# One gate convolution on Trainium2: its 144 input rows split as 128 rows times three shifts plus 16 rows loaded three times shifted

## The chip, the cores and the metric

The kernel runs on one core of one Trainium2 chip. The metric is the device time of one execution in microseconds (us). Three executions of the kernel before took 12310.65, 12336.9 and 12346.97 us; the median is 12336.9 us.

## The reference, cut to what matters

The input x has 32 images of 8 channels and 256x256 pixels. Two layers follow each other. Only layer 0 matters for the change; layer 1 is a group norm and a quantised 3x3 convolution of what layer 0 gives.

```
drive = gn(x); grid = drive
for _ in range(15):                                   # the lattice
    mapped = 3.9 * grid * (1 - grid)
    local = conv3x3_depthwise(mapped, K_local)
    grid = 0.85 * (0.7 * mapped + 0.3 * local) + 0.15 * drive
cml = clip(grid, 1e-4, 1 - 1e-4)
h   = relu(conv3x3(gn(x), Wp, bp))                    # the NCA: 8 -> 128 channels
nca = sigmoid(conv1x1(h, Wu, bu))                     # 128 -> 8
gin = concat([gn(x), cml, nca])                       # the gate: 24 channels
g   = sigmoid(conv1x1(relu(conv3x3(gin, Wg1, bg1)), Wg2, bg2))
y   = x + g * cml + (1 - g) * nca
```

The change touches `conv3x3(gin, Wg1, bg1)`, the gate's first convolution, 24 channels to 8.

## The kernel before, in words

**Groups.** The 32 images go in eight groups of four. The lattice of a group runs one channel of its four images at a time, 15 steps each, in two halves of two images (`half`, products at L499). While the lattice of group g runs, the products of the other stages are put between its halves: the NCA of the same group (`hidden` L585, `drain` L601), the gate of group g-1 (`gate`), and the group norm of group g+1. So the first group's lattice has no gate beside it, the next seven have 32 gate tiles each beside them, and the gates of the last four images stand alone at the end, before layer 1.

**Order.** The generators at the end of the stage write the order of TensorE's products by hand: each yields a weight, and `together` and `both` take the next piece from the one that is behind. The weights of the gate are not changed. The order on the other engines, and on the queue of DMA issues on SP, is not the program's: a planner with a cost model orders them by its own due times. So one tile's loads need not stand together on SP. Phase columns: the lattice leaves its columns sorted by phase, position q*64+j for column 4j+q, so that a shift by one column is a move by 64 positions for three phases and a move by 192 and one position for the fourth. This is why `PARTS` has five pieces for three shifts: 256, 192+63 and 192+63 columns.

**One gate tile** is 32 image rows, 8 tiles for each image, 256 in all. It works on eight blocks of four output rows. A block needs six input rows of 8 channels, 48 partitions for each of x, lattice and NCA. `inputs` (L656 to L665) loads them from the scratch `gs_s` in DRAM with three DMAs: x and lattice into `gin` (96 partitions), NCA into `gnc` (48 partitions), both from a pool with two buffers. The convolution (L758 to L768) then makes for each of the two sources, each of the five parts and each of four groups of 32 output partitions one product: 2 x 5 x 4 = 40. All of them read at most 512 columns in float32 and accumulate in one half of a PSUM tile. `S.activation` at L770 takes the sum into `r1`; the 1x1 convolution of the tile before (`opened`, L714 and L716) stands in PE's order just ahead of the 40 products, and the first of these waits for the activation L716.

**Loads and who needs them.** SP issues the tile's loads `gin`, `gnc` (L662), the tile's `mix` (L672), the NCA's `im` (L566), the store of y (L734), the lattice's loads and stores (L462), and the lattice's exchange of edge rows (L474 and L475, `m_a<-m_a`). The exchange comes after every second half: VectorE writes `m_a`, SP issues two small DMAs, and a half two places later on PE reads what they moved. SP takes its instructions strictly one after the other, in the order that the planner gave them.

Of the kernel before, what the change touches and what calls it, by code (L numbers as in the profile page):

```python
# [31 lines left out]
F32 = mybir.dt.float32  # L32
# [8 lines left out]
P = 128  # L41
C = 8
# [12 lines left out]
PART = PROWS * C * W  # L55
# [15 lines left out]
NT8 = 8  # L71
# [38 lines left out]
def kernel(  # L110
# [6 lines left out]
    wp: bass.AP,  # L117
    wu: bass.AP,
    wg1: bass.AP,
    wg2: bass.AP,  # L120
    w1: bass.AP,
    bp: bass.AP,
# [3 lines left out]
    nc = tc.nc  # L126
    B = x.shape[0]
    V, S, G, T = nc.vector, nc.scalar, nc.gpsimd, nc.tensor

    def dram_ap(t, offset, dims):  # L130
        return bass.AP(t.tensor, t.offset + offset, dims)


    cp = ctx.enter_context(tc.tile_pool(name="const", bufs=1))
# [8 lines left out]
    grp = cp.tile([P, 4], F32, name="grp")  # L143
    mean_x = cp.tile([P, B, 4], F32, name="mean_x")
    rstd_x = cp.tile([P, B, 4], F32, name="rstd_x")
    gw = cp.tile([96, 2, 3, 32], F32, name="gw")
    gw2 = cp.tile([P, P], F32, name="gw2")
    qw = cp.tile([P, 3, P], BF16, name="qw")
    wp_hi = cp.tile([P, 3, HID], F32R, name="wp_hi")
# [16 lines left out]
    with tc.tile_pool(name="prep", bufs=1) as pp, tc.tile_pool(name="prep2", bufs=2) as pp2:  # L166
# [3 lines left out]
        kc = pp.tile([P, 3, P], F32, name="kc")  # L170
        nc.sync.dma_start(kc, kcen)
        nc.sync.dma_start(gw, wg1)
        g2 = pp.tile([P, C], F32, name="g2")
        nc.sync.dma_start(g2, wg2)
        wl = pp.tile([P, 72], F32, name="wl")
# [79 lines left out]
    with ExitStack() as one:  # L255
# [7 lines left out]
        hp, xp, sp2, gp, gip = pool("hp", 4), pool("xp", 2), pool("sp2", 1), pool("gp", 3), pool("gip", 2)  # L263
# [4 lines left out]
        def unit():  # L268
            return ps_u.tile([P, 2, 512], F32, name="pt", tag="pt")
# [6 lines left out]
        fixed = lambda shape, name, dt=F32: np_.tile(shape, dt, name=name)  # L276
        hi, lo = fixed([P, 2, 2, W], "hi", F32R), fixed([P, 2, 2, W], "lo", F32R)
        ims = [fixed([P, 2, 8, PW], f"im{i}", F32R) for i in range(2)]
        for t in ims:
            for w in (0, PW - 1):  # L280
                G.memset(t[:, :, :, w].bitcast(F32), 0.0)
        TU = 2 * NT
        m_a = [fixed([P, TU, NJ + 2], f"m_a{i}") for i in range(2)]
        m_b = [fixed([P, TU, NJ + 1], f"m_b{i}") for i in range(2)]
        d_a = [fixed([P, TU, NJ], f"d_a{i}") for i in range(4)]
        d_b = [fixed([P, TU, NJ + 1], f"d_b{i}") for i in range(4)]
        for t in m_a:
# [104 lines left out]
        def lattice(g):  # L392
# [27 lines left out]
            def begin(ds, s):  # L420

                da, db = ds[s]
                for ts in (slice(0, 10), slice(10, TU)):
                    if s == 0:
# [55 lines left out]
            def half(c, step, s, d, m_a, m_b):  # L480
# [42 lines left out]
                if a2b:  # L523
                    edge = m_b[:, :, 0 : NJ + 1 : NJ]
                    G.tensor_tensor(edge, edge, junk.unsqueeze(1).to_broadcast([P, TU, 2]), ALU.mult)  # L525
                else:
# [129 lines left out]
        def inputs(b, t):  # L656

            src = gs_s[b % NBUF]
            gin = gip.tile([96, 8, W], F32, name="gin", tag="gin")
            gnc = gip.tile([48, 8, W], F32, name="gnc", tag="gnc")  # L660
            for j, to in enumerate((gin[:48], gin[48:], gnc)):
                nc.sync.dma_start(  # L662
                    to, dram_ap(src, j * PART + 32 * t * C * W, [[W, 48], [4 * C * W, 8], [1, W]])
                )
            return gin, gnc  # L665

        def blend(b, t):

# [25 lines left out]
        def begin_gate(b):  # L694
            return scales(b), (inputs(b, 0), blend(b, 0))

        PARTS = (
            (1, slice(0, 256), slice(0, 256)),
            (0, slice(64, 256), slice(0, 192)),
            (0, slice(1, 64), slice(192, 255)),  # L700
            (2, slice(0, 192), slice(64, 256)),
            (2, slice(192, 255), slice(1, 64)),
        )

        def gate(b):
# [36 lines left out]
            sc, ahead = staged.pop(b)  # L742
            last = None
            for t in range(NT8 + 1):
                while chores:
                    chores.pop(0)()
                now = {}
                two = unit()
                if last:
                    now["gt"] = opened(two[:, 1, :], last["r1"])  # L750
                    now["was"] = last
                if t < NT8:
                    (gin, gnc), mix = ahead
                    if t < NT8 - 1:
                        now["ahead"] = [inputs(b, t + 1)]
                    elif (b + 1) % GB:
                        staged[b + 1] = [inputs(b + 1, 0)]
                    pa = two[:, 0, :]  # L758
                    three = pa.rearrange("p (k w) -> p k w", w=W)
                    for j, src in enumerate((gin, gnc)):  # L760
                        rows_ = src.shape[0]
                        for n, (dx, to, of) in enumerate(PARTS):
                            for i in range(4):
                                T.matmul(  # L764
                                    three[32 * i : 32 * i + 32, :, to],
                                    gw[:rows_, j, dx, :], src[:, i::4, of],
                                    start=(j == 0 and n == 0), stop=(j == 1 and n == len(PARTS) - 1),
                                )  # L768
                    r1 = wk.tile([P, 512], F32, name="r1", tag="r1", bufs=1)
                    S.activation(r1, pa, AF.Relu, bias=bv[:, 0:1])  # L770
                    now["r1"], now["t"], now["mix"] = r1, t, mix

                def mix_(now):
                    was = now["was"]
                    was["y"] = mixed(now["gt"], *was["df"])

                def arrange_(now):
                    now["df"] = arrange(sc, now["mix"])

                def blend_(now):  # L780
                    if now["t"] < NT8 - 1:
                        now["ahead"].append(blend(b, now["t"] + 1))
                    elif (b + 1) % GB:
                        staged[b + 1] = scales(b + 1), (*staged[b + 1], blend(b + 1, 0))

                def measured_(now):
                    measured(now["was"]["t"], now["was"]["y"])

                def extremes_(now):
                    extremes(now["was"]["t"], now["was"]["y"])  # L790

                steps = []
                if last:
                    steps.append(mix_)
                if t < NT8:
                    steps += [arrange_, blend_]
                if last:
                    steps += [measured_, extremes_]
                chores.extend([lambda f=f, now=now: f(now) for f in steps])
                if sums:  # L800
                    chores.append(sums.pop(0))
                last = now
                yield 2.3 if t < NT8 else 0.9
                while t < NT8 - 1 and len(now.get("ahead", ())) < 2 and chores:
                    chores.pop(0)()
                ahead = now.get("ahead")
# [89 lines left out]
        for g in range(NG):  # L896
            fill, t = images(nca, g), T_NCA
            if g:
                fill, t = both(fill, t, after(g - 1, images(gate, g - 1)), T_GATE), t + T_GATE
            if g + 1 < NG:  # L900
                fill, t = both(fill, t, prep(g + 1), T_PREP), t + T_PREP
            if g == 0:
                fill, t = chain(prep(0, ((1,), (2,), (3,))), fill), t + 3.6
# [9 lines left out]
    with ExitStack() as two:  # L913
# [92 lines left out]
        for b in range(B + 1):  # L1006
# [5 lines left out]
            if last:  # L1012
                i, os_ = last
# [9 lines left out]
            if done:  # L1023
                i, os_ = done
# [53 lines left out]
```

## Time and profile before

The profiled execution of the kernel before took 12344.86 us; its span from first to last instruction is 12343.1 us.

| what | value |
|---|---|
| median of three executions | 12336.9 us |
| profiled execution, its span | 12344.86 us, 12343.1 us |
| TensorE busy | 11018.7 us, 89% of the span |
| VectorE busy | 7823.5 us, 63% |
| ScalarE, GpSimd busy | 3787.1 us (31%), 1577.6 us (13%) |
| mean granted TensorE clock | 0.950 |
| DMA queue of SP | 2380096 packets, 65.1% of 16 engines' span |
| stretch with lattice and gates side by side (1630 to 11396 us): TensorE, DMA share | 9164.00 of 9766.00 us, 0.69 |
| last gates alone (11396 to 11790 us): TensorE, DMA share | 314.41 of 394.00 us, 0.87 |

A line of the costliest groups reads: source line, engine, operation, what is written and read, shape (rows*columns of the array, then partitions x elements), count, and behind the bar busy time and mean time of one, then the engine's idle time before them and what ended it. A float32 product stands in the records as two instructions, so the gate's 40 products of a tile are 80 records.

### The profile page before, as it was taken

What the parts mean: (1) busy time and instruction counts of PE and PEld (TensorE: products, weight loads), DVE (VectorE), ACT (ScalarE), POOL (GpSimd) and SP (SyncE); (2) the same over time, 40 slices, a digit from 0 to 9 for tenths busy, and PEclk for the clock granted to TensorE, in tenths of its full rate; (3) what the DMA queues carried; (4) which work ended last, traced back from release to release, by engine and by line L of the source; (5) the groups of instructions that cost most, each with busy time, mean ns of one, the idle gap of its engine ahead of it and who ended that gap; (6) DMA issues with size and microseconds to landing.
All of it is one profiled execution on the core that took longest, in us unless ns stands there. A gap on an engine that the chain in (4) does not pass through costs nothing. (4 is left out here: it accounts for less than half of the span.)

```text
span 12343.1 us, 289997 instructions
## 1 busy us (share of the span) xinstructions
PE 11018.7 (89%) x124192; PEld 6195.1 (50%) x124192; DVE 7823.5 (63%) x11376; ACT 3787.1 (31%) x4034; POOL 1577.6 (13%) x2242
## 2 busy tenths in 40 slices
PE   4888899999999999999999999999999999999854
PEld 2554555555555555555555555555555555555222
DVE  4555666666666666666666666666666666665377
ACT  2222233332333333333333333333333333332133
POOL 1000011111111111111111111111111111111300
PEclk7999999999999999999999999999999999999676
DMA  6545567766777667676776667677667666665988
GB/s 169 98 96 100 102 136 144 144 137 139 142 145 147 137 135 147 144 144 130 147 147 139 133 140 148 135 144 148 134 142 149 137 132 126 125 121 115 201 246 257
DMA packets 2473159, 1759.74 MB, mean 143 GB/s; under 512 B 1021280, under 2 KB 2442944, under 8 KB 2471744
## 3 DMA queue, kind: packets, MB, share of 16 engines
q1 hardware_dynamic: 2380096, 1651.64, 65.1%
q10 hardware_dynamic: 91776, 89.53, 2.3%
q8 instruction: 979, 16.04, 0.6%
q14 instruction: 308, 2.52, 0.1%
HBM read 1130.62 MB, written 473.89 MB: 130 GB/s over the span
## 5 line engine op out<-in xcount | busy, mean ns | idle before, releaser
L593 ACT ACTIVATE h<-pt,bp_sb 128x1024 f32<-128x1024 f32 x2048 | 2274.2, 1112 | 5042.4 <-PE pt L585 5032.7
L499 PE MATMUL pt<-m_a,lw 64*64 64x325 f32 (+1 forms) x30720 | 2404.9, 432 | 405.2 <-DMA m_a<-m_a 358.0
L585 PE MATMUL pt<-im,wp_hi 48*128 48x512 f32 x12288 | 2627.7, 424 | 144.7 <-ACT h L593 105.2
L510 DVE SCALAR_TENSOR_TENSOR gt<-pt,d_b 128x650 f32<-128x650 f32 (+1 forms) x1920 | 1463.6, 763 | 1987.5 <-PE mark L274 1350.7
L510 DVE SCALAR_TENSOR_TENSOR gt<-pt,d_a 128x640 f32<-128x640 f32 (+1 forms) x1920 | 1446.9, 754 | 1608.5 <-PE mark L274 1137.5
L585 PE MATMUL pt<-im,wp_lo 48*128 48x512 f32 x12288 | 2437.3, 393 | 0.0
L499 PE MATMUL pt<-m_b,lw 64*64 64x320 f32 (+1 forms) x30720 | 2305.8, 417 | 111.8 <-DVE gt L510 79.6
L499 PEld LDWEIGHTS pt<-m_a,lw 64*64 64x64 f32 x30720 | 1459.6, 137 | 1193.0 <-issue 511.4
L499 PEld LDWEIGHTS pt<-m_b,lw 64*64 64x64 f32 x30720 | 1380.3, 133 | 903.0 <-issue 451.6
L585 PEld LDWEIGHTS pt<-im,wp_hi 48*128 48x128 f32 x12288 | 1160.8, 185 | 1250.9 <-issue 730.9
L520 DVE SCALAR_TENSOR_TENSOR m_a<-gt 128x640 f32<-128x640 f32 (+1 forms) x1792 | 1429.2, 798 | 58.6
L520 DVE SCALAR_TENSOR_TENSOR m_b<-gt 128x650 f32<-128x650 f32 (+1 forms) x1792 | 1384.3, 774 | 100.6 <-DVE gt L510 1.8
L525 POOL TENSOR_TENSOR m_b<-m_b,junk 128x36 f32<-128x36 f32 x896 | 243.5, 272 | 8070.3 <-DVE m_b L520 5355.6
L585 PEld LDWEIGHTS pt<-im,wp_lo 48*128 48x128 f32 x12288 | 1166.4, 186 | 201.1
L601 PE MATMUL acc<-h,wu_z 128*32 128x512 f32 x8192 | 1107.0, 611 | 0.0
L764 PE MATMUL pt<-gin,gw 96*32 96x384 f32 (+2 forms) x10240 | 775.6, 452 | 197.2 <-ACT gate L716 181.2
L274 PE MATMUL mark<-qw 64*64 64x1 bf16 x5760 | 946.4, 164 | 0.0
L764 PE MATMUL pt<-gnc,gw 48*32 48x384 f32 (+2 forms) x10240 | 735.3, 430 | 0.0
L764 PEld LDWEIGHTS pt<-gin,gw 96*32 96x32 f32 x10240 | 313.3, 115 | 823.7 <-issue 422.0
L687 POOL TENSOR_TENSOR d<-mix 128x256 f32<-128x256 f32 x512 | 554.2, 1099 | 1254.1 <-DVE gate L722 866.6
L274 PEld LDWEIGHTS <-qw 64*64 64x64 bf16 x5760 | 631.5, 110 | 137.0 <-issue 0.6
L764 PEld LDWEIGHTS pt<-gnc,gw 48*32 48x32 f32 x10240 | 295.0, 109 | 423.0 <-issue 416.3
(110 smaller groups left out, 5940.8 us busy)
## 6 DMA issues: line engine op xcount, KB each, us to landing
im<-xp_s SPq DMA_DIRECT2D x1024, 384.0 KB
gin<-gs_s SPq DMA_DIRECT2D x512, 384.0 KB
mix<-gs_s SPq DMA_DIRECT2D x512, 384.0 KB
gnc<-gs_s SPq DMA_DIRECT2D x256, 384.0 KB
d_a<-gs_s SPq DMA_DIRECT2D x2048, 36.0 KB
yb<-y_s ACTq DMA_DIRECT2D x28, 2432.0 KB
xr<-in_x_dram SPq DMA_DIRECT2D x128, 512.0 KB
xp_s<-hi SPq DMA_DIRECT2D x256, 256.0 KB
```

The lines of the kernel that those rows point to most:

```text
L274: T.matmul(one_[HIGH], qw[HIGH, 0, HIGH], qw[HIGH, 0, 0:1], start=True, stop=True)
L499: T.matmul(pt[dst], lw[src, c, w, dst], rhs[src], start=first, stop=not first)
L510: V.scalar_tensor_tensor(gt.rearrange("p (u c) -> p u c", u=2), pt[:, :, : w * n], FLOOR, d[:, ts, :].rearrange("p (u t) j -> p u (t j)", ...
L520: V.scalar_tensor_tensor(to, gt, 1.0, gt, ALU.subtract, ALU.mult)
L525: G.tensor_tensor(edge, edge, junk.unsqueeze(1).to_broadcast([P, TU, 2]), ALU.mult)
L585: T.matmul(ph[:, i, :].rearrange("p (h w) -> p h w", w=W), w[64 * i : 64 * i + 48, dx, :], rhs[:, :, dx : dx + W], start=(dx == 0 and w is ...
L593: S.activation(h.rearrange("p i c -> p (i c)"), ph.rearrange("p i c -> p (i c)"), AF.Relu, bias=bp_sb)
L601: T.matmul(acc[32 * g : 32 * g + 32], wu_z[:, 24 - 8 * i : 56 - 8 * i], hs[4 * g + i], start=(i == 0), stop=(i == 3),)
L687: G.tensor_tensor(d[:, cols], mix[:, 1, k], mix[:, 2, k], ALU.subtract)
L764: T.matmul(three[32 * i : 32 * i + 32, :, to], gw[:rows_, j, dx, :], src[:, i::4, of], start=(j == 0 and n == 0), stop=(j == 1 and n == le ...
```

## The change

`gnc` goes. `gin` grows to all 128 partitions: 48 rows of x, 48 of the lattice, and the first four of the NCA's six rows (32 partitions). The NCA's last two rows (16 partitions) are loaded three times, each time with the column shift already made, into a new tile `gl` of 48 partitions: five DMAs, one for each entry of `PARTS`. Two `gl` tiles are taken in turn; they are fixed tiles, and the one column that a shift leaves open is set to zero once. The weights are laid out to match: `gw` is 128 x 3 x 32, and a new `gwl` is 48 x 32. A tile has 5 x 4 products on 128 rows and 4 products on 48 rows, 24 in place of 40, and eight load DMAs in place of three.

```diff
-    gw = cp.tile([96, 2, 3, 32], F32, name="gw")
+    gw = cp.tile([P, 3, 32], F32, name="gw")
+    gwl = cp.tile([48, 32], F32, name="gwl")
...
         nc.sync.dma_start(gw, wg1)
+        nc.sync.dma_start(gwl, wg1l)
...
+        gls = [fixed([48, 8, W], f"gl{i}") for i in range(2)]
+        for t in gls:
+            for w in (0, W - 1):
+                G.memset(t[:, :, w], 0.0)
...
-            gin = gip.tile([96, 8, W], F32, name="gin", tag="gin")
-            gnc = gip.tile([48, 8, W], F32, name="gnc", tag="gnc")
-            for j, to in enumerate((gin[:48], gin[48:], gnc)):
+            gin = gip.tile([P, 8, W], F32, name="gin", tag="gin")
+            for j, (lo_, hi_) in enumerate(((0, 48), (48, 96), (96, P))):
                 nc.sync.dma_start(
-                    to, dram_ap(src, j * PART + 32 * t * C * W, [[W, 48], [4 * C * W, 8], [1, W]])
+                    gin[lo_:hi_],
+                    dram_ap(src, j * PART + 32 * t * C * W, [[W, hi_ - lo_], [4 * C * W, 8], [1, W]]),
                 )
-            return gin, gnc
+            gl = gls[(NT8 * b + t) % 2]
+            for dx, to, of in PARTS:
+                nc.sync.dma_start(
+                    gl[16 * dx : 16 * dx + 16, :, to],
+                    dram_ap(
+                        src,
+                        2 * PART + (32 * t + 4) * C * W + of.start,
+                        [[W, 16], [4 * C * W, 8], [1, of.stop - of.start]],
+                    ),
+                )
+            return gin, gl
...
-                    for j, src in enumerate((gin, gnc)):
-                        rows_ = src.shape[0]
-                        for n, (dx, to, of) in enumerate(PARTS):
-                            for i in range(4):
-                                T.matmul(
-                                    three[32 * i : 32 * i + 32, :, to],
-                                    gw[:rows_, j, dx, :], src[:, i::4, of],
-                                    start=(j == 0 and n == 0), stop=(j == 1 and n == len(PARTS) - 1),
-                                )
+                    for n, (dx, to, of) in enumerate(PARTS):
+                        for i in range(4):
+                            T.matmul(
+                                three[32 * i : 32 * i + 32, :, to],
+                                gw[:, dx, :], gin[:, i::4, of], start=(n == 0), stop=False,
+                            )
+                    for i in range(4):
+                        T.matmul(
+                            three[32 * i : 32 * i + 32], gwl, gl[:, i::4, :], start=False, stop=True
+                        )
...
-    wg1 = np.zeros((96, 2, 3, 32), np.float32)
-    for src, at, j in ((0, 0, 0), (1, 48, 0), (2, 0, 1)):
+    wg1 = np.zeros((P + 16, 3, 32), np.float32)
+    for src, at in ((0, 0), (1, 48), (2, 96)):
         for ro in range(4):
             to = C * ro
-            wg1[at + to : at + to + 24, j, :, to : to + C] = g5[src].reshape(24, 3, C)
+            wg1[at + to : at + to + 24, :, to : to + C] = g5[src].reshape(24, 3, C)
+    wg1l = wg1[P:].transpose(1, 0, 2).reshape(48, 32)
+    wg1 = wg1[:P]
```

More of the change, by code (lines that the diff above doesn't have):

```diff
@@ L119 @@
     wg1: bass.AP,
+    wg1l: bass.AP,
     wg2: bass.AP,
@@ L752, in gate @@
                 if t < NT8:
-                    (gin, gnc), mix = ahead
+                    (gin, gl), mix = ahead
                     if t < NT8 - 1:
@@ L1060 @@
         "wg1": wg1,
+        "wg1l": wg1l,
         "wg2": rep(a(L0_conv_Wg2).reshape(C, C).T),
```

## The prediction

> **What bounds the kernel now.** I read the page's busy shares first, then the costliest groups, then the stretches of the span, the waits, and last the order in time around one gate tile. A difference of 0.3% (37 us) is about what a measurement of this kernel can tell from none.
>
> The page, busy shares and the two groups that the change replaces:
>
> ```profile
> PE 11018.7 (89%) x124192; PEld 6195.1 (50%) x124192; DVE 7823.5 (63%) x11376; ACT 3787.1 (31%) x4034; POOL 1577.6 (13%) x2242
> ...
> L764 PE MATMUL pt<-gin,gw 96*32 96x384 f32 (+2 forms) x10240 | 775.6, 452 | 197.2 <-ACT gate L716 181.2
> ...
> L764 PE MATMUL pt<-gnc,gw 48*32 48x384 f32 (+2 forms) x10240 | 735.3, 430 | 0.0
> ```
>
> PE is the engine nearest to full, and the second source costs it as much as the first although it has half the rows. By stretches (length, then busy time of each engine, granted clock, DMA share, GB/s): lattice and gates side by side, then the last gates alone.
>
> ```profile
> 1630.00:11396.00 9766.00, 9164.00 (x106646) 5198.08 (x106638) 6304.76 (x9384) 3060.37 (x3198) 1329.81 (x1880) 0.98 0.69 139
> 11396.00:11790.00 394.00, 314.41 (x2924) 106.70 (x2924) 146.70 (x250) 72.21 (x100) 113.75 (x146) 0.69 0.87 198
> ```
>
> In the long stretch PE is busy for 93.8% at clock 0.98, so its order of work sets the time. PE's waits there, in all 602 us of idle time, by cause (us, times, longest):
>
> ```profile
> PE pt L499 <- DMA m_a<-m_a: 205.6, 112, 7.2
> PE pt L764 <- ACT gate L716: 159.4, 195, 0.9
> PE pt L585 <- ACT h L593: 91.2, 74, 2.0
> ```
>
> The largest is the lattice's exchange, a DMA: the one wait that the change can feed. The order in time on PE around one tile (start, length, and idle before):
>
> ```profile
> 4897.11 2.79 PE L764 MATMUL pt<-gin,gw 96*32 96x512 f32 x40 [0.81 <-ACT gate L716]
> 4899.82 2.78 PE L764 MATMUL pt<-gnc,gw 48*32 48x512 f32 x40
> 4902.53 0.99 PE L499 MATMUL pt<-m_a,lw 64*64 64x325 f32 x11
> ```
>
> A source takes 2.71 us from start to next start; then the lattice goes on without a gap.
>
> **The Trainium skill.** "TensorE: Matmul & The Clock Gate", section "Why this matters for your kernels", says that a product on 32 rows takes as long as one on 128: filling empty rows is free. The trace agrees between 96 and 48 rows (2.71 us each); 128 rows with 32 columns stand in it too (L601, below). The same page, Part 1, has TensorE fall to half rate after idle windows; in the last stretch the chain shows L764 at 10.64 us for 80 records where the full clock takes 5.43. "DMA: Bandwidth & Descriptors", section "Specifications", wants transfers of 512 B or more for full rate. In the packet records a 1024-byte packet took 78.6 ns and a 256-byte one 22.7 ns on the mean between 3000 and 9000 us: a little dearer per byte when undisturbed (medians of the fast ones 46 and 18), not twice. The same page, section "Queues, rings and completion order", says that each engine takes descriptors in ring order, so a small DMA stands behind a large one. The trace agrees: an exchange alone lands 2.7 us after its issue (median), one issued 2 to 4 us after a tile's last input load 4.4 us.
>
> **The change part by part.**
>
> *Products.* The 20 on `gin` get 128 rows and stay at 2.71 us. The 20 on `gnc` (2.71 us) go. Four products of 512 columns on 48 rows come. Their price: 16 records of L601 (128 rows, 32 columns, 512 elements) stand from 5054.69 to the next work at 5056.54, 1.85 us, so four products (8 records) 0.93; the first four of `gin` start their next weight load 0.89 us later. I take 0.89. Saving for a tile: 2.71 - 0.89 = 1.82 us at full clock. For the 224 tiles beside the lattice: 408 us. Should 128 rows with the strided source be slower than 96 the gain falls; nothing in the trace points to that, and the bound from L601 is 4% of 2.71, 0.11 us or 25 us in all.
>
> *Loads, bytes.* `gnc` was 384 packets of 1024 B. Now 256 of 1024 B in `gin`, and in `gl` 128 of 1024, 256 of 768 and 256 of 252 B. Beyond the equal count of 1024-byte ones that is 256 x 59 ns (768/1024 of 78.6) + 256 x 22.7 = 20.9 us over 16 engines = 1.3 us a tile; share 0.69 to about 0.74 with the shorter span. No engine waits for DMA bandwidth at that level; what matters is who stands behind it.
>
> *Loads, issues.* Five more on SP at 0.47 us (median of this line's issues): 2.35 us a tile, 602 us in all on a queue whose 11254 issues take 6120 us. SP waits idle 2988.7 us for `m_a` alone in the long stretch, so on the mean there is room. Behind the new issues stand, on SP, whatever the planner puts there: mix loads, y stores, lattice loads (no one waits soon), and exchanges, for which PE waits. SP also waits now and then for older loads before it issues more (85 + 90 us for `gin` and `gnc` ahead of L462); five more in flight feed this.
>
> *Exchanges.* I matched each exchange between 1640 and 11390 us (774) with its landing and with the half on PE that reads it; the difference is its slack. With a delay d for an exchange, PE loses what d exceeds the slack.
> (a) 256 exchanges have a gate tile between their half and its reader. That cover shrinks by 1.82 us. 28 have no slack now. Loss: 66 us.
> (b) 143 were issued within 14 us after a tile's last input load, none of them covered by a gate tile, 63 already without slack. If each comes d later: 87 us at d = 1.3 (the bytes alone), 133 at 1.8, 197 at 2.4 (the issues, undiminished). From below: 39 us, if only the 38 within 6 us are met. SP mostly waits for VectorE when an exchange comes (issued 2.62 us after its half in the median), so issues are partly hidden; I take 90.
> Together 156 us. Stalls also give the next exchanges time, which the sum leaves out.
>
> *New wait.* The four `gl` products wait for five DMAs more. Behind them on PE stands the next lattice half. The first input load is issued 38.4 us before its tile in the median, 13.6 at the 5th percentile; `gnc` lands 8.1 us after its issue, 16.1 at the 95th. Landing later by 2.35 + 1.3 is covered by some 25 us; without cover each late tile would cost up to those 3.7 us. I take 0, and 50 us as the upper end (13 such tiles).
>
> *Last gates alone.* 32 tiles in 364 us from 11415.5, 11.4 each. Nine of them are bound by PE at the low clock: 14.2 us, of which L764 10.64. They lose 3.6 us of products, to 10.7. The others lie at 7.2 to 11.6 with the queue at 0.87. DMA work is 0.84 (share from 11500 to 11780 us) x 11.4 = 9.6 us a tile, and grows by 1.1 to 1.3 to about 10.8. So tiles of 14.2 come down to the DMA's pace and those of 10 go up to it: 32 x 10.8 = 346. Gain 18 us; between -20 (waits at each image's start grow) and +60.
>
> *Start.* One small load, four strided memsets on GpSimd, before the first products: 0 to 2 us. Buffers: `gl` needs the bytes that `gnc` held.
>
> Sum against the profiled execution: 12345 - 408 - 18 + 156 = 12075; the median of the runs lies 8 below it: 12067.
>
> **Rivals.** *Second, the exchanges eat more.* Every input group holds back each exchange behind it by the whole 2.4 us, and the gate's cover goes: 197 + 66, and 30 of `gl` waits; no gain at the end. 12337 - 408 + 293 = 12222. For it: 63 of the 143 have no slack. Against it: SP is usually early.
> *Third, PE takes all of it.* Stalls only move, and the end gains 40: 12337 - 448 = 11889. For it: the 0.94 busy share. Against it: the 28 + 63 exchanges without slack, which set PE's pace where they stand.
> *Fourth, slower: the planner and the queue.* With eight loads for a tile the planner spreads them on SP (it already puts `gin` and `gnc` of one tile up to 81 us apart), and every exchange, not only those near, comes later. Over all 774 the loss is 242 us at d = 1.3, 401 at 1.8, 637 at 2.4. With the cover's 66 against the 426 gained it is even at d = 1.7 (366) and slower by over 0.3% from 1.8 on; at 2.4 it ends at 12337 - 426 + 703 = 12614. Against it: 576 of the exchanges stand over 30 us from an input load.
> That the change does not do what it says has no room: 24 products are in the program in place of 40, and PE's order is fixed.
>
> **How the numbers follow.** First case 0.62 (its own bounds: 11975 with a loss of 39 + 66 and a gain of 60 at the end, 12175 with 133 + 66, 25 for the rows and -20 at the end), second 0.18, third 0.10, fourth 0.08; 0.02 for a balance between second and fourth. The range holds the first, most of the second and the nearer part of the third: 11905 to 12250. Faster by over 0.3% (below 12300): 0.89. Within 0.3%: 0.03. Slower: 0.08, the fourth.
>
> **What would show it.** L764: 10240 records on 128 rows with busy time near 775 us and 2048 on 48 rows near 260. PE busy near 10530 us. The wait of L499 for `m_a` up from 358 to about 500 us; if near 650, the second case, if unchanged, the third. SP near 12500 issues and 6700 us. Last gates alone near 375 us with the DMA share above 0.9. The prediction is wrong if the 128-row products take longer than 2.8 us a tile, if `gl` shows up as a wait of L764, or if exchanges far from any input load lose their slack.

## The result, and the profile after

The changed kernel takes 12642.6 us (median of four executions, 12634.58 to 12651.85) against 12333.9 us for the kernel before beside it (12310.65 to 12346.97). The ratio is 1.0253, 95% interval 1.0235 to 1.027: 2.5% slower, where 2.2% faster was predicted. The profiled execution has a span of 12646.6 us, against 12343.1 before, and a mean granted clock of 0.929 against 0.950.

The page of the changed kernel, TensorE's busy time and the two groups that matter:

```profile
PE 10749.2 (85%) x116000; PEld 6091.9 (48%) x116000; DVE 7805.1 (62%) x11376; ACT 3788.2 (30%) x4034; POOL 1561.6 (12%) x2246
...
L506 PE MATMUL pt<-m_a,lw 64*64 64x325 f32 (+1 forms) x30720 | 2600.1, 460 | 938.6 <-DMA m_a<-m_a 882.2
...
L779 PE MATMUL pt<-gin,gw 128*32 128x384 f32 (+2 forms) x10240 | 780.4, 454 | 265.3 <-ACT gate L733 160.2
```

The products did what they were bought for: the 20 on 128 rows take as long as the 20 on 96 rows did (780.4 us against 775.6), and the 735.3 us on `gnc` are replaced by this group:

```profile
L784 PE MATMUL pt<-gl,gwl 48*32 48x512 f32 x2048 | 274.2, 606 | 4.2 <-DMA gl<-gs_s 4.2
```

Yet TensorE's busy time falls only by 269.5 us, not by the 456 that these groups give, because the lattice's products on `m_a`, which nothing changed, now take 2600.1 us. In the kernel before the same group reads:

```profile
L499 PE MATMUL pt<-m_a,lw 64*64 64x325 f32 (+1 forms) x30720 | 2404.9, 432 | 405.2 <-DMA m_a<-m_a 358.0
```

The loss is in the long stretch with lattice and gates side by side, and in it alone. From the first gate tile to the last beside the lattice it is 10078.3 us after (1630.1 to 11708.5) and 9763.7 before (1632.5 to 11396.2), 314.6 more; the last gates alone, from first start to last start, take 342.3 us in place of 347.5. The stretch after, in the columns that the prediction showed for before (length, busy times of PE, PEld, DVE, ACT, POOL, clock, DMA share, GB/s):

```profile
1630.00:11715.00 10085.00, 8982.05 (x99515) 5122.55 (x99507) 6296.30 (x9388) 3061.43 (x3197) 1328.85 (x1880) 0.95 0.71 140
```

TensorE was busy for 93.8% of it and now is for 89.1%, at clock 0.95 in place of 0.98. Its waits there (total, times, longest):

```profile
PE pt L506 <- DMA m_a<-m_a: 734.9, 222, 9.6
PE pt L779 <- ACT gate L733: 160.2, 196, 0.9
PE pt L592 <- ACT h L600: 80.0, 70, 1.9
```

The second and third are what they were. The first, the wait for the lattice's exchange of edge rows, was 205.6 us in 112 waits. The question is why the exchange is late, and whether it is the only thing that is.

**One late exchange.** SP's order in time in the changed kernel around one tile's loads (start, length, what, how many):

```profile
1812.43 1.26 SPq L469 DMA_DIRECT2D d_a<-gs_s  x3
1813.73 1.46 SPq L668 DMA_DIRECT2D gin<-gs_s  x3
1815.24 2.34 SPq L674 DMA_DIRECT2D gl<-gs_s  x5
1818.37 0.62 SPq L481 DMA_DIRECT2D m_a<-m_a  x1
1820.07 0.61 SPq L482 DMA_DIRECT2D m_a<-m_a  x1
```

VectorE's last write of the `m_a` that this exchange moves:

```profile
1812.14 0.69 DVE L527 SCALAR_TENSOR_TENSOR m_a<-gt 128x512 f32<-128x512 f32 x1
```

And TensorE, with the half that reads what the exchange brings:

```profile
1818.32 0.39 PE L592 MATMUL pt<-im,wp_lo 48*128 48x512 f32 x2
1824.78 1.79 PE L506 MATMUL pt<-m_a,lw 64*64 64x325 f32 x11 [6.06 <-DMA m_a<-m_a]
```

VectorE is done at 1812.83. SP has eight input loads ahead of the exchange and ends the last of them at 1817.58. It then stands still to 1818.37, and once more to 1820.07 before the second half of the exchange. In the records of completions the first `gin` load, eight issues before the exchange's first DMA, has landed at 1818.29, and the second, eight before its second, at 1820.06. The whole trace shows it: completions of SP's DMAs are counted on eight semaphores in turn, and of the 89 exchanges that stand directly behind a complete group of eight loads, 56 start within 0.3 us of the landing of the load eight places before, and 72 of their second halves. So the exchange leaves 5.5 us after VectorE: for 4.7 of them SP is still issuing the loads, for 0.8 it stands still. It lands at 1824.6 behind the `gl` loads (the last at 1824.28), and TensorE loses 6.06 us. Then comes a second price: the first records of the half take 1.79 us in place of 0.99, because the clock fell during the wait (the granted share is 1.00 up to 1822.0 us and 0.50 from there to 1828.8).

SP's waits on the whole, before:

```profile
SPq L474 <- DVE m_a L520: 3410.0, 741, 14.5
```

and after:

```profile
SPq L481 <- DVE m_a L527: 2564.5, 577, 14.0
SPq L469 <- DMA im<-xp_s: 327.3, 181, 3.8
SPq L469 <- DMA gin<-gs_s: 268.4, 227, 3.5
```

Before, SP mostly waited for VectorE when an exchange came: 741 times for the first DMA of one. After, only 577 times; in the others SP comes late. The order itself has changed little: in both kernels 89 exchanges stand directly behind a complete input group, and most tiles' loads stand together on SP in both (217 groups of eight after, 230 of three before, of 256). What stands in front of them is longer.

### The profile page after: what moved, and what is told of

It is laid out like the page before. It is cut to its first block, busy times and chain, and to the rows that moved or that the text cites. A ratio compares the mean times of both kernels' runs of the same rounds, so it can differ in the third digit from the quotient of the medians.

```text
span 12646.6 us, 275272 instructions
## 1 busy us (share of the span) xinstructions
PE 10749.2 (85%) x116000; PEld 6091.9 (48%) x116000; DVE 7805.1 (62%) x11376; ACT 3788.2 (30%) x4034; POOL 1561.6 (12%) x2246
## 5 line engine op out<-in xcount | busy, mean ns | idle before, releaser
L506 PE MATMUL pt<-m_a,lw 64*64 64x325 f32 (+1 forms) x30720 | 2600.1, 460 | 938.6 <-DMA m_a<-m_a 882.2
L592 PE MATMUL pt<-im,wp_hi 48*128 48x512 f32 x12288 | 2641.0, 426 | 132.9 <-ACT h L600 94.2
L506 PEld LDWEIGHTS pt<-m_a,lw 64*64 64x64 f32 x30720 | 1580.1, 146 | 1840.1 <-issue 1212.6
L592 PE MATMUL pt<-im,wp_lo 48*128 48x512 f32 x12288 | 2446.0, 394 | 0.0
L592 PEld LDWEIGHTS pt<-im,wp_hi 48*128 48x128 f32 x12288 | 1169.5, 186 | 1257.0 <-issue 730.3
L592 PEld LDWEIGHTS pt<-im,wp_lo 48*128 48x128 f32 x12288 | 1174.5, 187 | 201.7
L779 PE MATMUL pt<-gin,gw 128*32 128x384 f32 (+2 forms) x10240 | 780.4, 454 | 265.3 <-ACT gate L733 160.2
L779 PEld LDWEIGHTS pt<-gin,gw 128*32 128x32 f32 x10240 | 320.1, 116 | 878.1 <-issue 530.0
L1005 PE MATMUL pt<-qt,qw 128*128 128x512 bf16 (+1 forms) x864 | 232.8, 432 | 234.2 <-ACT ob L1010 234.2
L702 ACT ACTIVATE f<-mix,sc 128x512 f32<-128x512 f32 x256 | 208.3, 814 | 731.8 <-DVE y L740 441.0
```

Source lines behind the costliest of these rows:

```text
L506: T.matmul(pt[dst], lw[src, c, w, dst], rhs[src], start=first, stop=not first)
L592: T.matmul(ph[:, i, :].rearrange("p (h w) -> p h w", w=W), w[64 * i : 64 * i + 48, dx, :], rhs[:, :, dx : dx + W], start=(dx == 0 and w is ...
L702: S.activation(f, flat(mix[:, 0]), AF.Identity, bias=sc[:, 0:1], scale=sc[:, 2:3])
L779: T.matmul(three[32 * i : 32 * i + 32, :, to], gw[:, dx, :], gin[:, i::4, of], start=(n == 0), stop=False,)
L1005: T.matmul(pt[:, i:j, :], w[:, dx, :], qt[b % 2][h][:, k0 + i : k0 + j, dx : dx + W], start=(dx == 0), stop=(dx == 2),)
```

## The experiments

All times are medians of four executions; the ratio is to the kernel before, run beside it on the same chip. "Worth" turns the ratio into us on 12334. "Exchange wait" is TensorE's whole wait for `m_a<-m_a`. The letters in the quoted expectations name the theories that stand in the same text; they do not run on from one group to the next.

| kernel | us | ratio, 95% interval | worth, us | exchange wait, us |
|---|---|---|---|---|
| before | 12333.9 | 1 | 0 | 358.0 |
| after | 12642.6 | 1.0253 (1.0235 to 1.027) | +312 | 882.2 |
| eq_bytes | 12216.5 | 0.9907 (0.9889 to 0.9924) | -115 | 585.6 |
| small_gl | 12281.5 | 0.994 (0.9921 to 0.996) | -74 | 590.6 |
| one_gl | 12453.4 | 1.0076 (1.0051 to 1.01) | +94 | 723.3 |
| before_loads | 12950.0 | 1.0485 (1.0462 to 1.0508) | +598 | 743.6 |
| noex_before | 12047.4 | 0.977 (0.9749 to 0.979) | -284 | none |
| noex_after | 11569.2 | 0.9381 (0.9361 to 0.9401) | -763 | none |
| gl_pool | 12541.3 | 1.0154 (1.0132 to 1.0177) | +190 | 718.4 |
| in_act_before | 12432.6 | 1.0086 (1.006 to 1.0112) | +106 | 317.5 |
| in_act_after | 12585.0 | 1.0202 (1.0176 to 1.0227) | +249 | 472.0 |
| inim_act_after | 12778.8 | 1.0362 (1.0334 to 1.0389) | +446 | 616.4 |
| ex_pool_before | 13154.6 | 1.067 (1.0652 to 1.0687) | +826 | 880.8 |
| ex_pool_after | 13132.8 | 1.0656 (1.0639 to 1.0672) | +809 | 1127.1 |
| ex_act_after | 13100.3 | 1.0628 (1.0612 to 1.0644) | +775 | 371.8 |
| place_before | 12637.9 | 1.0235 (1.0219 to 1.025) | +290 | 433.6 |
| place_after | 12797.6 | 1.0357 (1.0334 to 1.0379) | +440 | 850.6 |
| place2_before | 12503.0 | 1.0131 (1.0104 to 1.0158) | +162 | 376.8 |
| place2_after | 12546.4 | 1.0161 (1.0146 to 1.0176) | +199 | 630.8 |

**Is the exchange all that stands in the way?** In both kernels it is left out.

```diff
-                else:
-                    exchange(m_a)
```

> The kernel before without the exchange of edge rows after every second half: this part of the lattice is left out, its two small DMAs are not issued, and the edge rows that the next half reads are the old ones. All theories: the 358 us of waits for m_a go, and with them the slow halves that follow long waits (69 us in the trace of before); 11880 to 11950 us.

> The changed kernel without the exchange, as in noex_before. Theory A (the exchange is the only thing between the products' saving and the time): the 882 us of waits and the 264 us of slow halves go, 11450 to 11520 us, 400 to 440 us below noex_before. Theory B (other waits, for gin, h or the gate's activations, would take the saving anyway): a difference of 100 to 300 us.

Measured: 12047.4 and 11569.2 us. The change is then worth -478 us, more than the 426 that the prediction gave its products. In the long stretch alone (first gate tile to last beside the lattice) it is 9687.8 us against 9197.0: 491 less, of which 409 are the gate's own products, about 40 the faster halves on `m_a` and the rest shorter waits. TensorE's waits without the exchange, in the changed kernel, longest first:

```profile
PE pt L1003 <- ACT ob L1008: 227.9, 28, 10.7
PE pt L777 <- ACT gate L731: 162.3, 193, 1.5
PE pt L590 <- ACT h L598: 119.9, 83, 2.7
PE pt L777 <- DMA gin<-gs_s: 113.8, 32, 15.7
```

The first belongs to layer 1, after the gates; the others are about as in the full kernel. TensorE is busy for 10441.2 us here and for 10957.5 without the exchange before the change. The difference lies above the 400 to 440 us of theory A and far from theory B: without the exchange nothing takes the saving. This shows the way by which the loss reaches TensorE. It does not show how SP and the DMA engines divide it, for SP is also freed here of its waits for VectorE (2564.5 us in the changed kernel). Both levels came higher than expected, by 97 and 49 us above their ranges; other waits grow where the exchange's go (in noex_before `h` for L583 from 105.2 to 133.8 us, `gt` for L499 from 92.8 to 104.7). In the same units the exchange costs the kernel before 284 us and the changed one 312 + 763 = 1075 us. It is this that the change made dearer, by 791 us.

**The products alone.** The changed kernel with only the first of the five `gl` pieces: as many packets of 1024 bytes as before (1152 a tile), four loads in place of three, the same 24 products.

```diff
-            for dx, to, of in PARTS:
+            for dx, to, of in PARTS[:1]:
```

> The changed kernel, of whose gl only the unshifted piece is loaded: four loads a tile and exactly the 1152 packets of 1024 B of the kernel before, 24 products. The two shifted parts of gl stay zero, so their share of the convolution is left out. If places and bytes in SP's queue are the whole loss: 11980 to 12120 us, exchange wait 350 to 450 us. Theory D (the shorter gate no longer covers the exchange, whatever is loaded): 12230 to 12350 us, exchange wait over 550, as the saving goes into the waits.

Measured: worth -115 us, with this as the largest wait:

```profile
PE pt L505 <- DMA m_a<-m_a: 585.6, 202, 11.9
```

So of some 426 us less than 120 arrive even where hardly anything is added to the DMA queue. The quicker gate, with one load more, raises the exchange's wait by 228 us. This is what theory D said, 14 us better than its range; that places and bytes are the whole loss is refuted.

**Bytes and number of loads.** one_gl has all the bytes of `gl` in one unshifted load; small_gl keeps all five loads but makes each 4 columns wide; before_loads adds the five loads to the kernel before, into rows of `gnc` that no product reads.

```diff
-            for dx, to, of in PARTS:
-                nc.sync.dma_start(
...
+            nc.sync.dma_start(gl, dram_ap(src, 2 * PART + 32 * t * C * W, [[W, 48], [4 * C * W, 8], [1, W]]))
```

> The changed kernel, with gl loaded by one DMA of 48 rows of 1024 B in place of five pieces: the same bytes (393 KB), the same 24 products, but four loads a tile in place of eight. The two shifts are not made, so this part of the convolution reads unshifted columns. Theory A (in flight: the ninth DMA of SP waits until the first of eight has landed, and eight loads of a tile use up all places in front of an exchange): 11990 to 12120 us, the wait of the lattice's products for the exchange falls from 882 to about 450 us. Theory B (the 261 KB more a tile hold back the exchange in the rings): stays at 12600 to 12650, wait near 880. Theory D (the shorter gate no longer covers the exchange): stays at 12600 to 12650 as well.

```diff
-                    gl[16 * dx : 16 * dx + 16, :, to],
+                    gl[16 * dx : 16 * dx + 16, :, to.start : to.start + 4],
```

> The changed kernel with eight loads a tile, but each of the five pieces of gl only 4 columns wide: some 10 KB in place of 392 KB. The rest of gl stays zero, so most of this part of the convolution is left out. Theory A (places in flight): still slow, 12350 to 12600 us, the exchange wait 600 to 850 us; somewhat less than the full one, since the first input load lands sooner with less beside it. Theory B (bytes): 11950 to 12080, exchange wait under 400. Theory C (only SP's time for five more issues, 2.35 us a tile): 12550 to 12650, since the issues are all there.

```diff
-            gnc = gip.tile([48, 8, W], F32, name="gnc", tag="gnc")
+            gnc = gip.tile([96, 8, W], F32, name="gnc", tag="gnc")
...
+            for dx, to, of in PARTS:
+                nc.sync.dma_start(
+                    gnc[48 + 16 * dx : 64 + 16 * dx, :, to],
...
```

> The kernel before with its 40 products, and the five shifted loads added: eight loads a tile, into 48 further partitions of gnc that nothing reads. Theory A: PE keeps its 5.43 us a tile and pays for the exchanges on top: 12850 to 13050 us, exchange wait 800 to 950. Theory D (the shorter gate is needed for the loss): 12340 to 12450, exchange wait near 400. Theory B (bytes): 12600 to 12900; here even more bytes are added (392 KB).

Measured: from eq_bytes, the bytes cost 209 us (one_gl), four more loads with few bytes 41 us (small_gl), and both together 427 us (after). The 41 and the 427 are not on equal ground, though. small_gl carries 121 KB a tile less than eq_bytes, and the pieces of 768 and 252 bytes in after take more DMA time than the whole rows of one_gl: for each gate tile of the long stretch the packets of all DMAs took 468 us together in small_gl, 479 in eq_bytes, 506 in one_gl and 514 in after. If the cost goes in proportion to this time (an estimate from these figures), the bytes of after are worth some 270 us and four more loads some 120, about 395 of the 427. That bytes and loads cost more together than singly is therefore not shown. Nor did any single theory hold in these runs: one_gl lies between theory A (at most 12120 us) and theories B and D (at least 12600), small_gl between B (at most 12080) and A (at least 12350), and before_loads has the time of theory A with a shorter exchange wait than A said. before_loads shows that the loads need no quicker gate to do harm: +598 us with the products of before (here the bytes come on top of all of `gnc`, so it is more than the change adds).

**Is it the place on SP's queue?** First only the five `gl` loads leave SP, to GpSimd:

```diff
-                nc.sync.dma_start(
+                nc.gpsimd.dma_start(
                     gl[16 * dx : 16 * dx + 16, :, to],
```

> The changed kernel with the five loads of gl issued from GpSimd in place of SP: bytes and products as in the changed kernel, three input loads a tile on SP as before. Theory A and theory C (SP's places or SP's time): 11950 to 12150 us, exchange wait 350 to 500. Theory B and theory D: 12550 to 12650. GpSimd is busy 12% of the span; if its own order of work is held up by the loads, the waits for its subtractions (d, f, lo) and for the edge product of m_b grow and some of the gain is lost.

Measured: worth +190 us, 122 better than after, and still slower than before; GpSimd's busy time rises from 1561.6 to 2241.0 us. Theories A and C, at most 12150 us, fail; B and D, 12550 to 12650, come out within 9 us. The exchanges that have the first load of an input group under 16 us before them, and no gate tile between them and their reader, show why (means in us over the same 177 of the long stretch, the set of the table of exchanges further down but for one):

| kernel | VectorE's last write to issue | issue to landing | sum |
|---|---|---|---|
| before | 0.11 | 3.95 | 4.06 |
| eq_bytes | 0.41 | 4.65 | 5.06 |
| small_gl | 1.49 | 3.87 | 5.36 |
| one_gl | 0.63 | 5.42 | 6.05 |
| gl_pool | 0.48 | 5.81 | 6.29 |
| after | 2.34 | 4.70 | 7.04 |

With `gl` issued elsewhere the exchange is issued nearly at once, and then takes longer to land. Of the 3.0 us by which it lands later than before, 1.0 are there already in eq_bytes, and only some 0.75 go when `gl` leaves SP's queue. This speaks for the time on SP being in large part no loss of its own: on SP or on the DMA engines, the exchange waits for the same bytes.

Then all the gate's inputs, and with inim_act_after the NCA's too, leave SP for ScalarE (the same word changed from sync to scalar at each load):

```diff
-                nc.sync.dma_start(
+                nc.scalar.dma_start(
                     gin[lo_:hi_],
```

> Control for in_act_after: the kernel before with the gate's three input loads issued from ScalarE, 3 x 0.61 = 1.8 us of ScalarE a tile in place of 4.9. Theory Q (the exchange is late because it stands behind inputs on SP's own queue; what in_act_after did not gain was lost on ScalarE): the exchange wait falls below 358, to 200 to 280 us, the waits for h and for VectorE rise by 50 to 150 us, time 12300 to 12450. Theory S (what delays it is shared by both queues): exchange wait 330 to 450 us, time 12400 to 12600.

> The changed kernel with all eight gate input loads issued from ScalarE, 8 x 0.61 = 4.9 us of ScalarE a tile. Theory Q (SP's own queue): the exchange wait falls from 882 to 350 to 500 us, time 12000 to 12250. Theory S (shared by both queues): exchange wait 650 to 900 us, time 12400 to 12700. In both theories ScalarE's activations for h and the gate come later: their waits on TensorE rise by 50 to 200 us, which is in the figures.

> The changed kernel with the gate's inputs and the NCA's loads issued from ScalarE. Theory Q: nothing but mix loads, stores and the lattice's own DMAs are left on SP; exchange wait 150 to 350 us, time 11850 to 12150, below both kernels. Theory S: exchange wait 600 to 900 us, time 12350 to 12700.

Measured: the waits of in_act_after.

```profile
PE pt L506 <- DMA m_a<-m_a: 472.0, 165, 12.2
...
PE pt L779 <- ACT gate L733: 194.3, 224, 9.5
PE pt L731 <- ACT r L788: 159.5, 46, 7.6
PE pt L592 <- ACT h L600: 156.9, 103, 5.0
PE pt L506 <- DVE gt L517: 131.7, 93, 6.7
```

The exchange wait falls by 410 us, into the range of theory Q. The time does not follow (12585 where at most 12250 was expected), because what depends on ScalarE comes late: the waits for `h` at L592 rose by 62.7 us, for the lattice's `gt` by 69.7 and for `r` by 118.8. The estimate of 50 to 200 us for this was too low, and its reason was wrong too. An issue of these loads took 0.31 us on ScalarE (median), not 0.61, which is what another DMA takes there (`xp_s<-zt`). But 680.6 us of ScalarE's idle time ahead of `h`, and 269.1 ahead of `r`, now end with the landing of an earlier gate load; part of this time would have been idle anyway. The control in_act_before has a time of theory Q's range, and an exchange wait between the two theories. With the controls the change costs 143 us where ScalarE issues the inputs (in_act_after less in_act_before) and 312 where SP does, and it adds 155 us of exchange wait (317.5 to 472.0) in place of 524. So about half of the loss goes when the inputs leave SP for ScalarE. That it goes because of SP's queue is not shown: ScalarE also spreads the loads (1.37 us from one `gl` load to the next in the median, 0.47 on SP), so that fewer bytes stand in front of an exchange at a time. And how much of the other 143 us is ScalarE's lateness, and how much the DMA engines that both queues share, was not separated. For the exchanges of the table, VectorE's last write to issue is 0.13 us in in_act_before and 0.30 in in_act_after, issue to landing 3.52 and 4.39. The Trainium skill, "DMA: Bandwidth & Descriptors", section "Issuing engines are not separate DMA queues", says that such DMAs run on the same 16 engines whoever starts them and that a second issuer saves only the time of issuing. That agrees with both moves: the exchange is issued almost at once (0.30 and 0.48 us in place of 2.34), and the landing stays long (4.39 and 5.81 in place of 4.70). inim_act_after loses more: its exchange wait is up again at 616.4 us, so the NCA's loads from ScalarE did not help the exchange, against theory Q. It has no control, and why they did not is open.

The opposite, moving the exchange off SP:

```diff
-                nc.sync.dma_start(t[0::16, :, below], t[14::16, :, above])
+                nc.gpsimd.dma_start(t[0::16, :, below], t[14::16, :, above])
```

(and its second line; in ex_act_after with the word scalar).

> The control: the kernel before with the exchange issued from GpSimd. If the exchange's place is what turns the change from a gain into a loss, this one gains only the 200 to 350 us of its own exchange waits (12000 to 12150), and the changed kernel with the same move is 300 to 450 us faster than this one, the saving on PE. If the move helps both alike, the difference between them stays at +300.

> The changed kernel as it is, but the exchange's two DMAs are issued from GpSimd, so that they stand neither behind SP's places nor behind the loads on SP's rings. If the loss lies in the exchange's place in SP's queue: 11750 to 12000 us, the exchange wait below 300 us (the kernel before had 358 even with three loads). If the loads reach PE by another way (inputs that land late, loads of im, the clock): over 12300 us. Risk for both: GpSimd waits for m_a in its own order and holds up d, f and lo; then these waits grow and the time lies between.

> The changed kernel with the exchange issued from ScalarE's queue: rings of its own, but ScalarE then waits for m_a ahead of activations that PE needs. If the exchange's place is the cause: exchange wait below 300 us, but waits for the activations L600, L788 and L733 grow; 11800 to 12300 us. If it is not the cause: over 12500.

Measured: all three lose over 6%, far above the times that were expected if the exchange's place is the cause. From GpSimd the exchange is late on its own account (880.8 us of waits in the kernel before the change), and the change is then worth -17 us in place of +312, a hint that the loss arises where exchange and loads share a queue, no more. From ScalarE the exchange wait is down to 371.8 us, and other waits take its place:

```profile
PE pt L592 <- ACT h L600: 272.0, 323, 4.6
PE pt L779 <- DMA gin<-gs_s: 261.5, 63, 14.8
...
PE pt L592 <- DMA im<-xp_s: 158.6, 63, 15.3
```

**A better place on SP.** The inputs of the next gate tile are put in the program right behind the second exchange of a pair, where no exchange follows at once; in place2 the NCA's `im` loads too.

```diff
                     exchange(m_a)
+                    if step % 2 and wanted:
+                        wanted.pop(0)()
...
-                        now["ahead"] = [inputs(b, t + 1)]
+                        now["ahead"] = [None]
+                        want(lambda to=now["ahead"], t=t: to.__setitem__(0, inputs(b, t + 1)))
```

> The control of the first run: the kernel before with only the three input loads in that place. Exchanges behind inputs wait 112 us in it now, and the clock adds some 30: 12200 to 12320 us.

> The changed kernel with the same loads and products, but a tile's eight input loads are put right behind the second exchange of a pair (the first is one half earlier, the next two or three halves later), not at the start of the gate tile. Theory E (the loss comes from loads that stand shortly ahead of an exchange in SP's order, by places, bytes and the shorter distance together): the waits of the exchanges behind inputs (416 us, and 110 of low clock after them) mostly go: 12150 to 12350 us, exchange wait 450 to 600. If the five more loads cost their time wherever they stand: 12550 to 12650.

> The control: the kernel before with both groups of loads in that place. It has 358 us of exchange waits and about 69 of low clock after them to lose: 12050 to 12250 us. Under theory E the changed kernel in this place is then faster than this one by most of the 408 us on PE (250 to 400); if the change's loads cost time by themselves, it is not faster.

> As the run before, and the NCA's four loads of im put in the same place, one of the two groups behind each second exchange. Theory E: the exchanges behind im, which lost their cover to the shorter gate, get free too: 11900 to 12200 us, exchange wait 150 to 400. If not: within 50 us of the run before.

Measured: all four are slower than before, so the place did not mend the kernel and the expectation that it would failed. Inputs are late instead: `gin` makes TensorE wait 186.9 us in place_after and 226.5 in place2_after, against 105.0 in after. Two things can be read nevertheless. In place2 the change costs some 40 us in place of 312, but both kernels are slower than before. And the first group, which has no gates, ends its lattice sooner: the first gate tile starts at 1511 us in place2_before and at 1632 before (1631 in place_before, where `im` stays), so the NCA's loads hold back exchanges as well. The later groups give it back. The waits for `gin` do not explain all of it, and what else makes these four slow is open. No version that computes all of the reference was found that beats the kernel before.

## Why the prediction was wrong, by its steps

**Products** held, a little under the size. 20 products of 128 rows cost what 96 rows did. The four on `gl` take 0.99 us from first start to next start, not 0.89, so a tile's products take 3.71 us in place of 5.43: 1.72 us saved, not 1.82. Over the 224 tiles that is 387 us (1227.0 to 840.2), not 408, and the pair without the exchange shows that it can arrive in full.

**Loads, bytes** and **Loads, issues**: right as counts (12535 issues of SP), wrong in what was made of them. The packets of 768 and 252 bytes took 80.3 and 42.3 ns on the mean, where 59 and 22.7 were put in: 31.4 us of packet time a tile in place of 20.9, so 2.0 us over 16 engines in place of 1.3. The share rose to 0.71 only, because the stretch got longer. The issues were priced at 0.47 us each, as if SP could always go on issuing. With eight loads in a row it cannot: the exchange directly behind them waits, in most cases, until the first of the eight has landed. The prediction had seen such waits ("SP also waits now and then for older loads") and gave them no price.

**Exchanges** is where the sum failed. The same 774 exchanges of the long stretch, matched one to one between the two kernels, with TensorE's idle time ahead of their reader:

| exchanges | before, us | after, us | difference | predicted | eq_bytes, difference |
|---|---|---|---|---|---|
| covered by a gate tile (256) | 20 | 165 | +145 | 66 | +72 |
| first input load under 16 us before (178) | 112 | 416 | +304 | 90 | +109 |
| others (340) | 79 | 170 | +91 | 0 | +65 |
| sum | 211 | 751 | +540 | 156 | +246 |

*(a) The cover* was right as a term: +72 us in eq_bytes, where little but the cover changed, against 66. In the full change the exchange is later at the same time, and the two add up to 145.

*(b) Behind inputs* is the step that failed most, mis-sized by more than three (the 90 us were said of 143 exchanges, chosen a little more narrowly). It put in that the exchange comes 1.3 to 2.4 us later, and took 90 us because SP is usually early. Measured, it lands 3.0 us later: SP issues it 2.2 us later, and it takes 0.75 us longer to land. Counted in the prediction's own way, as what the delay exceeds the slack by, a delay of 2.9 us gives about 330 us for these exchanges (an estimate from the slacks in the trace of before), near the 304. So the way of counting was right and the delay was not. Two terms were left out. The issue stalls until earlier loads have landed. And the exchange itself comes sooner after the loads when the gate's products are shorter: VectorE's last write is 11.6 us after the group's first load before, 10.5 in eq_bytes (medians), so that more of the loads is still in front of it. It lands 1.0 us later in eq_bytes, where the DMAs move the bytes of before; that fits the +109, though eq_bytes has one load more as well.

*The others*, far from inputs, were taken as safe. They lose 91 us, 65 of it in eq_bytes already. That the lattice's own loads and the NCA's `im` loads stand in front of them, and that TensorE needs the rows sooner, fits; it was not taken apart.

**The clock**, a term that the sum didn't have. The prediction cited "TensorE: Matmul & The Clock Gate", Part 1, for the last stretch alone. Each long wait has the same effect in the middle of the kernel: the next half on `m_a` takes 2.38 us as a rule, 1.0 us more after a wait of 2 to 3.4 us, 1.86 more after 3.4 to 5 us and 1.97 more above. There were 30 waits of 2 us or more, now 144. Over all, the halves behind exchanges were 69 us longer than the rule and are now 264: +195 us, which is the 2600.1 against 2404.9 us of the groups above. The page's section "HAM oscillation" describes just this, a wait for a DMA that throttles the next burst, with a window of about 3.4 us; here waits under it already cost half of the price.

The sum of the measured terms is -387 + 540 + 195 = +348 us for the long stretch. TensorE's other waits there are some 40 us shorter (for `gt` 69.1 to 40.5, for `h` 91.2 to 80.0), which leaves 308; the stretch grew by 314.6.

**New wait** held at about nothing (4.2 us for `gl`; `gin` rose from 16.0 to 105.0 us, all of it in the last gates). **Last gates alone** gained 5 us where 18 was said; in eq_bytes, with the bytes of before, they gain 47 (300.8 us), and small_gl, with eight loads of few bytes, ends at the same 300.8, so the added bytes set their pace. **Start** cost nothing that shows: the first gate tile stands 2 us earlier.

Of the rivals the second had the right mechanism in the main and stopped at 293 us, with no term for the clock. The fourth came nearest in time and sign, 12614, and is wrong in its reason, so its number is luck: the planner did not spread the loads (217 of 256 tiles have all eight in a row). It asked for a delay of 2.4 us on every exchange; in fact 178 exchanges near inputs took more than half of the loss, and the clock added another 195 us. The 0.08 for slower was too little for a term, the exchange, that the prediction itself had found at zero slack in 91 places.

## What to carry to other kernels

A small transfer on which the busiest engine waits can take the whole worth of a change: ask first what the change does to it, and price the wait with what follows it, a stalled queue in front and a slower clock behind. Price loads that are added ahead of such a transfer by the time until they have landed, not by the time to issue them. No way round it was found here: moved to GpSimd, the loads still held up the landing; moved to ScalarE, they held up its results. A shorter burst of products takes away cover, and it brings the next small transfer closer to the large ones that were started at the burst's beginning; with equal bytes some 426 us of products were worth 115 here.

## What was unexpected of the hardware

- A DMA issue on SP stood still until the DMA eight issues earlier had landed (behind complete groups of eight loads: 56 of 89 first halves and 72 of 89 second halves of exchanges, within 0.3 us). This is how the program counts completions, on eight semaphores in turn; the profile shows it as SP waiting for `gin` ahead of `m_a`.
- Waits of 2 to 3.4 us on TensorE already brought the slow clock to part of the next 2.38 us, 1.0 us more on the mean; waits of 3.4 us or more 1.9 us.
- Packets of 768 bytes took 80.3 ns on the mean in the changed kernel, as long as those of 1024 bytes (78.4); packets of 252 bytes took 42.3, those of 256 bytes, which belong to other DMAs, 22.3.
- ScalarE needed 0.31 us (median) for each gate load that it issued, SP 0.47 us for the same `gin` loads. Its results came late all the same: 949.7 us of its idle time ahead of `h` and `r` ended with the landing of an earlier gate load.
